# A conv-and-attention pair on one core: sampled keys copied by ScalarE, PSUM pools in another order, first queries copied by bank, one store moved on GpSimd's queue

## The chip, the cores and the metric

The kernel runs on one core of one Trainium2 chip. A core has four compute engines that run at the same time, each through its own list of instructions in order: TensorE (PE in the profile; its weight loads are shown as PEld), VectorE (DVE), ScalarE (ACT) and GpSimd (POOL). SyncE (SP) issues DMA transfers; GpSimd and ScalarE also issue some. The engines wait for each other through semaphores. Matmul results land in PSUM, a small memory of eight banks, from which VectorE or ScalarE has to copy ("evict") them.

The metric is the device time of one execution, in microseconds (us), as the median of several runs. Lower is better.

## What is computed

All numbers are float32. The input x has shape (2, 512, 32, 32). Two layers follow each other. The first is a deformable attention with an MLP behind it:

```python
xn  = bn(x, bn1_g, bn1_b)
q   = gconv1x1(xn, qw)                              # 8 groups of 64 channels
off = depthwise_conv6x6(q, stride=4)                # 8 x 8 positions for each image and group
off = tanh(pointwise(gelu(off + b), 2)) * 4
kv  = grid_sample(xn, grid + off)                   # 64 sampled keys for each image and group
k, v = gconv1x1(kv, kw), gconv1x1(kv, vw)
pos  = sign(d) * log1p(abs(d)),  d = grid_q - grid_kv          # 1024 queries x 64 keys x 2
bias = relu(relu(pos @ w1 + b1) @ w2 + b2) @ w3 + b3           # an MLP of width 128
x  = x + out_w @ (softmax(q k / 8 + bias) v) + out_b
x  = x + mlp_w2 @ gelu(mlp_w1 @ bn(x, bn2_g, bn2_b) + b) + b
```

The second layer is plain attention over the 1024 positions with 512 channels (Wq, Wk, Wv, Wp), added to x. By far the most work is the bias: an MLP with a hidden layer of 128 x 128 for every pair of a query and a key, 16 times over (two images, eight groups).

## The kernel before

**Opening.** A few matmuls on zeros (`wake`, L147) keep TensorE busy until the first input is there. Then the first 128 channels go through `chain(0)`: the batch norm on ScalarE (L264), the queries on TensorE into a PSUM tile `psq` of two banks (L270), and four copies of them into `qa` (L276). Output groups are numbered f = 0, 1 and lie in bank f; halves of the pixels h = 0, 1 lie in the upper and lower 64 partitions. VectorE then applies the 36 taps of the strided convolution (L308, L310), ScalarE the GELU (L342), TensorE the pointwise product (L354), ScalarE the tanh (L364). The features of the positions (`fe`) go to DRAM (`fdr`, L405, issued by SP) and come back broadcast to all partitions (`fb`, L579, issued by SP right behind it). From `fb` ScalarE and VectorE make the tables `ta` and `tb` (L590, L596), and from these VectorE makes `h`, the first hidden layer of the bias MLP (L610).

Meanwhile TensorE multiplies weights of the second layer with each other (`weights`, L533). The products are copied by ScalarE into `gs` (L539) and stored to DRAM by a DMA of 1 MB that GpSimd issues (`gdr`, L540). `rank`, `order` and `arrange` sort the hidden units by the sign of their last weight; the last part of it is a handful of very small GpSimd operations on `sc`, `w3f` and `w3u` (L242 to L248).

**Main loop.** 256 steps follow, each for four keys of one group. In a step TensorE computes four blocks of the second hidden layer (L627, eight matmuls each, operands `h` and `cw`). Each block lies in one tile of the PSUM pool `zp`, which has three buffers of two banks. ScalarE evicts the blocks with a ReLU (`rx` at L634, `ua`, `uo` or `ub` at L636), VectorE adds them in pairs (L644), accumulating DMAs issued by GpSimd and copies issued by SP add them further (L646, L658, L661, L663), and once in four steps TensorE multiplies the sums by the last layer (L692) into a tile of the PSUM pool `simp` (two buffers of one bank). VectorE makes `h` two steps ahead, in three buffers.

**Behind the loop.** One slice of other work is put into each step: the generator `later()` yields the rest of `chain` and `sample` for the other channels, and its slices are placed behind the second eviction of the step with `issue_after`. `sample(ci)` computes the sampled keys, eight times in all. ScalarE makes interpolation weights (L446, L449) and scales the batch-norm bias in place (L452), VectorE multiplies the weights (L454), and TensorE sums over the pixels into `pkv`, which is a tile of `zp` like the blocks (L462). VectorE evicts `pkv` in four operations with the batch-norm scale and bias, which also put the keys into the order in which the loop takes them (L475). TensorE then makes k and v from `kv` (`pkk` at L482, `pkv` at L484), and ScalarE copies these (L488, L490). A scheduler reorders instructions between engines by their dependencies, so the order on each engine is that of the built program, and not always that of the text.

**Afterwards.** The output projection (`project`, L872) uses `zp`. Then the pools `simp` and `zp` are closed and a pool `mq` of four buffers of two banks takes all eight banks for the MLP (L925) and the second layer (L1056, L1154).

The change touches these lines:

```python
zpp, simpp = (tc.tile_pool(name=n, bufs=c, space=PSUM) for n, c in (("zp", 3), ("simp", 2)))     # L132
copy = nc.vector.tensor_copy if ci == 0 and h == 1 else nc.scalar.copy                           # L275
nc.vector.scalar_tensor_tensor(                                                                  # L475
    d[:, e], v[:, e], bns[r, k : k + 1], u[:, e], ALU.mult, ALU.add)
nc.gpsimd.dma_start(out=gdr[i], in_=gs[:, i])                                                    # L540
```

Of the kernel before, what the change touches and what calls it, by code (L numbers as in the profile page):

```python
# [8 lines left out]
F32 = mybir.dt.float32  # L9
AF = mybir.ActivationFunctionType  # L10
ALU = mybir.AluOpType
AX = mybir.AxisListType
PSUM = bass.MemoryType.PSUM

P = 128
# [4 lines left out]
J = 64  # L20
# [26 lines left out]
def conv_seq_kernel(ctx: ExitStack, tc: tile.TileContext, x, xt, kst, pst, cst, vec, wsm, outw, w1, w2, wl, wlt, brow, out):  # L47
    nc = tc.nc
# [11 lines left out]
    def col(name, i=0):  # L60
        return vs[:, VOFF[name] + i : VOFF[name] + i + 1]

    bns = cp.tile([P, 8], F32, name="bns")
# [65 lines left out]
        x = [q[:, k : k + 2, n : n + 512] for k in (0, 2) for n in (0, 512)]  # L129
        return w + [wsum[:, j] for j in range(3)], x + [parts[:, j] for j in range(3)]  # L130

    zpp, simpp = (tc.tile_pool(name=n, bufs=c, space=PSUM) for n, c in (("zp", 3), ("simp", 2)))  # L132
    zp, simp = zpp.__enter__(), simpp.__enter__()

    def flat(name):
        return zp.tile([P, 2, 512], F32, tag="ps2", name=name).rearrange("p h n -> p (h n)")
# [3 lines left out]
    ph = php.__enter__()  # L140
    with tc.tile_pool(name="lp", bufs=2) as lp:


        def wake(src, n):
            ps = flat("wake")
            for _ in range(n):
                nc.tensor.matmul(ps[0:32, 0:512], src[:, 0:32], src[:, 0:512], start=True, stop=True)  # L147


        edge = ph.tile([P, 2], F32, name="edge")  # L150
# [7 lines left out]
        for n in range(2):  # L158
            idle = lp.tile([P, 4 * HW], F32, tag="h1", name="idle", bufs=3)
            nc.gpsimd.memset(idle[:, 0:512], 0.0)  # L160
            wake(idle, n + 1)
        cs = ph.tile([P, 202], F32, name="cs")
        ws = ph.tile([P, 1408], F32, name="ws")
        wq, wk = ws[:, 0:512], ws[:, 512:1024]
# [85 lines left out]
        def newest(engine):  # L250
            return next(i for i in reversed(nc.cur_bb.bb.instructions) if i.engine == engine)
# [4 lines left out]
        def chain(ci):  # L256
# [3 lines left out]
            for i in range(K):  # L260
                k = k0 + i
                if i == 0:
                    xn = xn0.pop()
                nc.scalar.activation(xn, xn, AF.Identity, bias=col("bn1b", k), scale=bns[:, k : k + 1])  # L264
                if ci > 0:
                    yield
                ps = flat("psq")

                for f_, h_, f, h in QUADS:
                    nc.tensor.matmul(  # L270
                        ps[h_, f * 512 : (f + 1) * 512], wq[f_, k * P + 64 * f : k * P + 64 * f + 64],
                        xn[f_, h * 512 : (h + 1) * 512], start=True, stop=True,
                    )
                for f_, h_, f, h in QUADS:
                    copy = nc.vector.tensor_copy if ci == 0 and h == 1 else nc.scalar.copy  # L275
                    copy(qa[f_, b, k, h * 512 : (h + 1) * 512], ps[h_, f * 512 : (f + 1) * 512])  # L276
                if i + 1 < K:
                    xn = load(b, k + 1)
                elif ci + 1 < len(CHAINS):
                    xn0.append(load(*CHAINS[ci + 1][0]))  # L280
                yield
# [29 lines left out]
            else:  # L311


                for m in range(3):
# [9 lines left out]
                    for y0, y1, t0, t1 in rows:  # L324
                        for k in range(K) if y1 - y0 < 8 else (slice(0, K),):
                            src, dst = pr[:, t0:t1, k, y0:y1, :], acc[:, m, k, y0:y1, :]
# [87 lines left out]
        def sample(ci):  # L414
            G = CHAINS[ci]
            K = len(G)
            th = state[ci]
            gx = th[:, 0:2].rearrange("p i g j -> p (i g j)")

            nc.vector.tensor_scalar(gx, gx, 1.0, 16.0, ALU.add, ALU.mult)  # L420
            if ci > 0:
                yield


            sg = ph.tile([P, 5, 2, K * J], F32, tag="fe", name="sg")
            hat = sg[:, 0:4].rearrange("p a f j -> p (a f j)")[:, 0 : 4 * K * J]
            nc.scalar.activation(hat, gx, AF.Abs, bias=edge[:, 0:1])
            nc.scalar.activation(hat, hat, AF.Relu, bias=edge[:, 1:2])
            nc.scalar.activation(hat, hat, AF.Relu, bias=1.0, scale=-1.0)
            yield  # L430
            nc.vector.tensor_tensor(sg[:, 4], sg[:, 0], sg[:, 1], ALU.mult)
            hx = ph.tile([P, 2, K, J], F32, tag="hx", name="hx")
            hxf = hx.rearrange("p f k j -> p (f k j)")
            nc.scalar.activation(hxf, th[:, 0].rearrange("p g j -> p (g j)"), AF.Abs, bias=hb[:, 0:1])
            nc.scalar.activation(hxf, hxf, AF.Relu, bias=1.0, scale=-1.0)
            yield
            gy = th[:, 1].rearrange("p (f k) j -> p f k j", f=2)
            for i, (b, k) in enumerate(G):
                g = b * NCH + k
                xnt = ph.tile([P, 8, P], F32, name="xnt")  # L440
                nc.sync.dma_start(out=xnt, in_=xt[:, b, k])
                wt = ph.tile([P, 8, 2, J], F32, name="wt")
                for t in range(8):
                    if t == 4:
                        yield
                    nc.scalar.activation(wt[:, t], gy[:, :, i, :], AF.Abs, bias=hb[:, 1 + t : 2 + t])  # L446
                yield
                wtf = wt.rearrange("p t f j -> p (t f j)")
                nc.scalar.activation(wtf, wtf, AF.Relu, bias=1.0, scale=-1.0)  # L449
                for f in range(2):  # L450
                    r, v = slice(64 * f, 64 * f + 64), sg[:, 4, f, i * J : (i + 1) * J]
                    nc.scalar.activation(v[r], v[r], AF.Copy, scale=col("bn1b", k)[r])  # L452
                yield
                nc.vector.tensor_tensor(  # L454
                    wt, wt, hx[:, :, i, :].unsqueeze(1).to_broadcast([P, 8, 2, J]), ALU.mult
                )
                yield
                ps = flat("pkv")
                for t in range(8):
                    for f in range(2):  # L460
                        r = slice(64 * f, 64 * f + 64)
                        nc.tensor.matmul(  # L462
                            ps[r, 0:J], xnt[:, t, r], wt[:, t, f, :], start=(t == 0), stop=(t == 7)
                        )
                kv = ph.tile([P, J], F32, name="kv")

                for f in range(2):
                    r = slice(64 * f, 64 * f + 64)
                    d = kv[r].rearrange("p (e i t) -> p e i t", e=2, t=8)
                    v, u = (  # L470
                        t[r].rearrange("p (i e t) -> p e i t", e=2, t=8)
                        for t in (ps[:, 0:J], sg[:, 4, f, i * J : (i + 1) * J])
                    )
                    for e in range(2):
                        nc.vector.scalar_tensor_tensor(  # L475
                            d[:, e], v[:, e], bns[r, k : k + 1], u[:, e], ALU.mult, ALU.add
                        )
                yield


                ps, pk = flat("pkv"), flat("pkk")
                nc.tensor.matmul(pk[:, 0:J], wk[:, k * P : (k + 1) * P], kv, start=True, stop=True)  # L482
                for f_, h_, f, h in QUADS:
                    nc.tensor.matmul(  # L484
                        ps[h_, f * 512 : f * 512 + 256], kv[f_, :], uo[f_, k, h * 256 : (h + 1) * 256],
                        start=True, stop=True,
                    )
                nc.scalar.activation(kz[:, g], pk[:, 0:J], AF.Copy, scale=DH ** (-0.5))  # L488
                for f_, h_, f, h in QUADS:
                    nc.scalar.copy(vp[f_, g, h * 256 : (h + 1) * 256], ps[h_, f * 512 : f * 512 + 256])  # L490
                yield
            state[ci] = None
# [34 lines left out]
        def weights(i):  # L527
            ps = [flat("psg") for _ in range(2)]
            for o in range(NCH):
                for k in range(NCH):  # L530
                    if i == 0 and (o, k) in ((1, 0), (3, 1)):
                        yield
                    nc.tensor.matmul(  # L533
                        ps[k // 2][:, k % 2 * 512 : k % 2 * 512 + 512], wls[i][:, 0, o, k * P : (k + 1) * P],
                        wls[i][:, 1, o, :], start=(o == 0), stop=(o == NCH - 1),
                    )
            yield
            for k2 in range(2):
                nc.scalar.copy(gs[:, i, 2 * k2 : 2 * k2 + 2, :].rearrange("p k o -> p (k o)"), ps[k2])  # L539
            nc.gpsimd.dma_start(out=gdr[i], in_=gs[:, i])  # L540


        PE = mybir.EngineType.PE
# [14 lines left out]
        for _ in head:  # L558
            pass
        with tc.issue_after(newest(mybir.EngineType.Activation)):  # L560
            next(g, None)
        with tc.issue_after(newest(PE)):
            arrange()
        with tc.issue_after(newest(PE)):
            next(n)
        next(n, None)


        NS = NG * NSL
# [274 lines left out]
    with ExitStack() as top, tc.tile_pool(name="wp", bufs=2) as wp:  # L844
# [164 lines left out]
        project(1, *op1, op1w[:, 3:5].rearrange("p a k n -> p a (k n)"))  # L1009
        spread([xb[:, j] for j in range(7)])  # L1010
        load_unit(*units[1])
        for pl in (simpp, zpp):
            pl.__exit__(None, None, None)
        mqp = tc.tile_pool(name="mq", bufs=4, space=PSUM)
        mq = mqp.__enter__()
# [326 lines left out]
```

## Time and profile before

| What | Value |
| --- | --- |
| Median of 3 runs | 2685.91 us (2681.35 to 2688.14) |
| Time of the profiled execution | 2688.11 us |
| Its span, first to last instruction | 2686.3 us |
| Mean granted TensorE clock | 0.997 |
| PE, DVE, ACT, POOL busy | 99%, 84%, 63%, 21% of the span |
| Main loop on PE (L627) | 1789.6 us busy, 16384 records |
| Eviction of the keys (L475) | 32 operations, 0.25 us each |

How to read it: a profile names for each instruction its engine, its line in the kernel, and its tiles as output<-input. In lists of waits, the columns are the total idle time of the engine, how often, and the longest. "PEclk" is the share of full speed that TensorE's clock was granted. A line in order of time gives the start and the length in us, then the instruction, how many records are merged in it (a float32 matmul has two), and in brackets the idle time of the engine just before it and what ended that.

### The profile page before, as it was taken

How to read it: one execution, taken by the hardware profiler on the slowest of the kernel's cores; microseconds unless marked ns; L12 is line 12 of the kernel's file. 1: busy time of each engine (PE TensorE's matmuls, PEld its weight loads, DVE VectorE, ACT ScalarE, POOL GpSimd, SP SyncE). 2: the span in 40 equal slices, each digit the busy share in tenths (PEclk: the TensorE clock that was granted, in tenths of full speed). 3: DMA queues.
4: the chain of work that ended last, by engine and by line, in shares of the span. 5: the costliest groups of instructions: out<-in, count | busy, mean ns of one | idle time of the engine just before them, and what ended most of it. 6: DMA issues, size and time to landing. Idle time of an engine off the chain costs nothing.

```text
span 2686.3 us, 46913 instructions
## 1 busy us (share of the span) xinstructions
PE 2663.3 (99%) x19596; PEld 960.0 (36%) x19596; DVE 2249.2 (84%) x1353; ACT 1688.3 (63%) x2193; POOL 576.9 (21%) x615
## 2 busy tenths in 40 slices
PE   9999999999999999999999999999999999999999
PEld 3343322332332333233323333333344444446455
DVE  6999999999999999999999999999774484466354
ACT  4787898788978888877777777777621131114041
POOL 1222222222222222222222222222243222000000
PEclk9999999999999999999999999999999999999999
DMA  5766766767666766666766776776631110000000
GB/s 197 150 150 145 163 139 141 158 140 157 147 147 142 153 144 142 145 140 142 150 146 146 149 150 142 151 149 145 153 123 47 47 47 33 15 16 0 32 0 32
DMA packets 96131, 316.67 MB, mean 118 GB/s; under 512 B 17104, under 2 KB 19424, under 8 KB 93232
## 3 DMA queue, kind: packets, MB, share of 16 engines
q0 software_dynamic: 57312, 202.26, 40.4%
q1 hardware_dynamic: 38176, 111.10, 11.6%
q8 instruction: 155, 2.54, 0.4%
q14 instruction: 56, 0.46, 0.0%
q10 hardware_dynamic: 432, 0.31, 0.0%
HBM read 74.28 MB, written 6.55 MB: 30 GB/s over the span
## 4 chain that ended last, share of the span: by engine, by line
PE 83%; DVE 6%; issue 5%; DMA 3%; ACT 2%; POOL 1%; DVEq 0%; SPq 0%; POOLq 0%; ACTq 0%
PE ps L627 52%; PE sw L925 14%; PE sw L1056 9%; DVE h L610 3%; PE sw L1154 2%; PE sim L692 2%; DMA ua<-ua 1%; DMA ua<-uo 1%; PE psg L533 1%; DVE ub L644 1%; PE sw L872 1%; DVE uo L644 1%; DVE ua L644 0%; ACT rx L634 0%; DMA wr<-in_wlt 0%
## 5 line engine op out<-in xcount | busy, mean ns | idle before, releaser
L627 PE MATMUL ps<-h,cw 128*32 128x512 f32 x16384 | 1789.6, 593 | 11.5 <-DVE kv L475 8.6
L610 DVE CUSTOM_DVE_ANT_1 h<-ta,tb 128x4096 f32<-128x4096 f32 (+1 forms) x257 | 1131.8, 4405 | 48.9 <-PE ps L627 45.0
L627 PEld LDWEIGHTS ps<-h,cw 128*32 128x32 f32 x16384 | 541.2, 110 | 1225.0 <-issue 1155.7
L634 ACT ACTIVATE rx<-ps,sc 128x1024 f32<-128x1024 f32 x512 | 568.3, 1110 | 177.2 <-PE ps L627 158.8
L636 ACT ACTIVATE ub<-ps,sc 128x1024 f32<-128x1024 f32 x256 | 308.2, 1204 | 97.2 <-PE ps L627 97.1
L644 DVE SCALAR_TENSOR_TENSOR ub<-rx,sc,ub 128x1024 f32<-128x1024 f32 x256 | 327.5, 1279 | 6.0 <-ACT ub L636 5.7
L646 POOL DMA_DIRECT2D ua<-ub x128 | 115.5, 903 | 730.4 <-DVE ub L644 703.3
L925 PE MATMUL sw<-xb,w1t 128*128 128x512 f32 x448 | 196.7, 600 | 3.1 <-DVE xs L123 3.1
L925 PE MATMUL sw<-hm,w2t 128*128 128x512 f32 x448 | 193.6, 592 | 0.0
L646 POOL DMA_DIRECT2D uo<-ub x127 | 117.0, 921 | 356.6 <-DVE ub L644 316.1
L636 ACT ACTIVATE ua<-ps,sc 128x1024 f32<-128x1024 f32 x128 | 154.1, 1204 | 54.6 <-PE ps L627 54.3
L663 POOL DMA_DIRECT2D ua<-uo x126 | 110.6, 878 | 352.5 <-DMA ua<-uo 350.7
L636 ACT ACTIVATE uo<-ps,sc 128x1024 f32<-128x1024 f32 x128 | 154.1, 1204 | 48.7 <-PE ps L627 45.9
L644 DVE SCALAR_TENSOR_TENSOR ua<-rx,sc,ua 128x1024 f32<-128x1024 f32 x128 | 163.7, 1279 | 13.7 <-ACT ua L636 13.7
L644 DVE SCALAR_TENSOR_TENSOR uo<-rx,sc,uo 128x1024 f32<-128x1024 f32 x128 | 163.8, 1280 | 7.8 <-ACT uo L636 7.7
L123 DVE TENSOR_TENSOR hm<-hm,sw 128x1024 f32<-128x1024 f32 x56 | 67.5, 1219 | 107.2 <-PE sw L925 106.9
L658 POOL DMA_DIRECT2D ua<-ua x126 | 153.8, 1221 | 1.6 <-issue 1.6
L925 PEld LDWEIGHTS sw<-xb,w1t 128*128 128x128 f32 x448 | 86.1, 193 | 112.6 <-issue 106.4
L934 ACT ACTIVATE hm<-hm,vs 128x512 f32<-128x512 f32 x64 | 42.6, 714 | 129.0 <-DVE hm L123 129.0
L925 PEld LDWEIGHTS sw<-hm,w2t 128*128 128x128 f32 x448 | 85.1, 190 | 107.1 <-issue 106.7
L123 DVE TENSOR_TENSOR xs<-xs,sw 128x1024 f32<-128x1024 f32 (+1 forms) x48 | 55.6, 1171 | 72.0 <-PE sw L1056 36.0
L1056 PE MATMUL sw<-aT,vt 128*128 128x512 f32 x224 | 96.7, 593 | 0.3 <-ACT aT L1136 0.3
(238 smaller groups left out, 1799.0 us busy)
## 6 DMA issues: line engine op xcount, KB each, us to landing
ua<-ub POOLq DMA_DIRECT2D x128, 512.0 KB, 4.9
uo<-ub POOLq DMA_DIRECT2D x127, 512.0 KB, 5.2
fb<-fdr SPq DMA_DIRECT2D x64, 512.0 KB, 5.2
ua<-ua POOLq DMA_DIRECT2D x126, 256.0 KB, 6.4
ua<-uo SPq DMA_DIRECT2D x126, 256.0 KB, 2.6
ua<-uo POOLq DMA_DIRECT2D x126, 256.0 KB, 3.8
w1t<-in_w SPq DMA_DIRECT2D x8, 1024.0 KB, 4.7
w2t<-in_w SPq DMA_DIRECT2D x8, 1024.0 KB, 4.7
```

Source lines behind the costliest of these rows:

```text
L123: nc.vector.tensor_tensor(out, a, b_, op)
L610: nc.vector._custom_dve(TENSOR_ADD_SAT, out=h1[:, y : y + step].rearrange("p y t x -> p (y t x)"), in0=a.unsqueeze(1).to_broadcast([P, ste ...
L627: nc.tensor.matmul(ps[32 * q : 32 * q + 32, h, :], cw2[:, 32 * z : 32 * z + 32], h1[:, 16 * h : 16 * h + 16, q, :], start=True, stop=True,)
L634: nc.scalar.activation(o, ps, AF.Relu, bias=sc[:, 4 + z : 5 + z])
L636: nc.scalar.activation(o, ps, AF.Relu, bias=sc[:, 4 + z : 5 + z], scale=sc[:, z : z + 1])
L644: nc.vector.scalar_tensor_tensor(r[1], r[0], sc[:, z : z + 1], r[1], ALU.mult, ALU.add)
L646: nc.gpsimd.dma_start(out=sums[s][1], in_=sums[s][3], accum_op=ALU.add)
L658: nc.gpsimd.dma_start(out=lanes(s, 0), in_=lanes(s, 1), accum_op=ALU.add)
L663: nc.gpsimd.dma_start(out=lanes(s, 1), in_=lanes(s + 1, 0), accum_op=ALU.add)
L692: nc.tensor.matmul(sims[gi][q : q + 32, :], w_, t[:, h, :], start=(i == 0 and f == 0), stop=(i == NSL // 4 - 1 and m == len(parts[e]) - 1),)
L925: nc.tensor.matmul(ps[:, m, :], w[:, a, k, m * P : (m + 1) * P], x[:, b_, k, :], start=(k == 0), stop=(k == 1),)
L1056: nc.tensor.matmul(ps[:, m, :], w[:, a, k, c + m * P : c + (m + 1) * P], x[b_][:, k, :], start=(k == 0), stop=(k == nk - 1),)
```

## The change

1. **Sampled keys.** `pkv` is now copied out of PSUM by one ScalarE operation with the batch-norm scale, for all 128 partitions at once and already in the loop's order. The scaled bias goes to a tile of its own, `uv`, in the same order, and one VectorE addition of 128 x 64 puts the two together.
2. **PSUM pools.** `simp` is opened before `zp` and closed after it, so that `simp` lies in the first two banks and `zp` in the other six.
3. **First queries.** Of the four copies out of `psq`, ScalarE takes those of f = 0 (bank 0), and VectorE those of f = 1 (bank 1). Before, the engines were split by h.
4. **Wake.** The last of the three matmuls on zeros has 256 columns in place of 512.
5. **G to DRAM.** `weights` yields once more before the DMA, so that the first `gdr` store stands on GpSimd's queue behind five of the seven small operations of `arrange`, just before the last two (L246). The second store stays where it was.

```diff
-    zpp, simpp = (tc.tile_pool(name=n, bufs=c, space=PSUM) for n, c in (("zp", 3), ("simp", 2)))
-    zp, simp = zpp.__enter__(), simpp.__enter__()
+    simpp, zpp = (tc.tile_pool(name=n, bufs=c, space=PSUM) for n, c in (("simp", 2), ("zp", 3)))
+    simp, zp = simpp.__enter__(), zpp.__enter__()
...
-        def wake(src, n):
+        def wake(src, *sizes):
             ps = flat("wake")
-            for _ in range(n):
-                nc.tensor.matmul(ps[0:32, 0:512], src[:, 0:32], src[:, 0:512], start=True, stop=True)
+            for n in sizes:
+                nc.tensor.matmul(ps[0:32, 0:n], src[:, 0:32], src[:, 0:n], start=True, stop=True)
...
-            wake(idle, n + 1)
+            wake(idle, *((512,), (512, 256))[n])
...
-                    copy = nc.vector.tensor_copy if ci == 0 and h == 1 else nc.scalar.copy
+                    copy = nc.vector.tensor_copy if ci == 0 and f == 1 else nc.scalar.copy
...
+                kv, uv = (ph.tile([P, J], F32, name=name) for name in ("kv", "uv"))
+                rowwise, natural = "p (e i t) -> p e i t", "p (i e t) -> p e i t"
                 for f in range(2):
                     r, v = slice(64 * f, 64 * f + 64), sg[:, 4, f, i * J : (i + 1) * J]
-                    nc.scalar.activation(v[r], v[r], AF.Copy, scale=col("bn1b", k)[r])
+                    nc.scalar.activation(
+                        uv[r].rearrange(rowwise, e=2, t=8), v[r].rearrange(natural, e=2, t=8), AF.Copy,
+                        scale=col("bn1b", k)[r],
+                    )
...
-                kv = ph.tile([P, J], F32, name="kv")
-
-                for f in range(2):
-                    r = slice(64 * f, 64 * f + 64)
-                    d = kv[r].rearrange("p (e i t) -> p e i t", e=2, t=8)
-                    v, u = (
-                        t[r].rearrange("p (i e t) -> p e i t", e=2, t=8)
-                        for t in (ps[:, 0:J], sg[:, 4, f, i * J : (i + 1) * J])
-                    )
-                    for e in range(2):
-                        nc.vector.scalar_tensor_tensor(
-                            d[:, e], v[:, e], bns[r, k : k + 1], u[:, e], ALU.mult, ALU.add
-                        )
+                nc.scalar.activation(
+                    kv.rearrange(rowwise, e=2, t=8), ps[:, 0:J].rearrange(natural, e=2, t=8), AF.Copy,
+                    scale=bns[:, k : k + 1],
+                )
+                nc.vector.tensor_tensor(kv, kv, uv, ALU.add)
...
                 nc.scalar.copy(gs[:, i, 2 * k2 : 2 * k2 + 2, :].rearrange("p k o -> p (k o)"), ps[k2])
+            yield
             nc.gpsimd.dma_start(out=gdr[i], in_=gs[:, i])
...
         with tc.issue_after(newest(mybir.EngineType.Activation)):
+            next(g)
+        with tc.issue_after(newest(PE)):
+            arrange()
+        with tc.issue_after(newest(mybir.EngineType.Pool)):
             next(g, None)
         with tc.issue_after(newest(PE)):
-            arrange()
-        with tc.issue_after(newest(PE)):
             next(n)
-        next(n, None)
+        for _ in n:
+            pass
...
-        for pl in (simpp, zpp):
+        for pl in (zpp, simpp):
             pl.__exit__(None, None, None)
```

## The prediction

> **What bounds the kernel.** I read the page first: busy time per engine, then who waits for whom on TensorE, then TensorE's clock by stretch, then instructions in order of time around each wait.
>
> ```profile
> PE 2663.3 (99%) x19596; PEld 960.0 (36%) x19596; DVE 2249.2 (84%) x1353; ACT 1688.3 (63%) x2193; POOL 576.9 (21%) x615
> ```
>
> TensorE is busy for 99% of the 2686.3 us span, so a change that removes none of its matmuls can gain only where it is idle or slow. The list of its waits adds up to 18.3 us; the largest (total, times, longest):
>
> ```profile
> PE ps L627 <- DVE kv L475: 8.6, 3, 3.6
> PE sw L925 <- DVE xs L123: 3.1, 1, 3.1
> PE wake L147 <- POOL idle L160: 1.6, 1, 1.6
> PE ps L627 <- ACT rx L634: 1.7, 4, 0.6
> PE ps L627 <- DVE h L610: 1.1, 1, 1.1
> ```
>
> Nearly half of the idle time is three waits for VectorE's eviction of the sampled keys (L475). Next, the granted clock in five stretches (PE, weight loads, DVE, ACT, POOL busy; then PEclk, DMA share, GB/s): the three key waits, the first MLP product, the opening.
>
> ```profile
> 533.60:537.90 4.30, 2.04 (x21) 0.49 (x17) 4.22 (x7) 1.11 (x1) 0.37 (x1) 1.00 0.63 124
> 840.60:846.60 6.00, 3.23 (x20) 0.60 (x16) 5.19 (x7) 1.26 (x3) 0.90 (x1) 0.72 0.48 113
> 1147.90:1157.70 9.80, 6.21 (x36) 1.61 (x32) 5.93 (x7) 3.96 (x4) 2.49 (x3) 0.65 1.00 237
> 1987.30:1996.50 9.20, 6.07 (x8) 2.52 (x8) 2.38 (x4) 0.00 (x0) 2.72 (x3) 0.63 0.94 336
> 6.70:37.70 31.00, 31.00 (x123) 14.04 (x122) 17.29 (x62) 10.25 (x19) 5.46 (x13) 1.00 0.71 271
> ```
>
> A clock of 0.72 over 6.00 us is 3.4 us at half speed, 0.65 over 9.80 is 6.9, 0.63 over 9.20 is 6.8; the 2.26 us wait in the first stretch costs no clock. So a long wait is paid twice. Around 843 us, TensorE, then VectorE:
>
> ```profile
> 835.28 5.36 PE L627 MATMUL ps<-h,cw 128*32 128x512 f32 x48
> 843.41 3.32 PE L627 MATMUL ps<-h,cw 128*32 128x512 f32 x16 [2.77 <-DVE kv L475]
> 846.65 0.43 PE L482 MATMUL pkk<-kv,ws 128*128 128x64 f32 x2
> 838.06 4.41 DVE L610 CUSTOM_DVE_ANT_1 h<-ta,tb 128x4096 f32<-128x4096 f32 x1
> 842.51 0.84 DVE L475 SCALAR_TENSOR_TENSOR kv<-pkv,bns,sg 64x32 f32<-64x32 f32 x4
> ```
>
> The product `pkv` was ready at 835.4, but its eviction stands behind a 4.41 us layer-1 pass on VectorE, which runs without a gap; meanwhile `pkv` holds one of three PSUM buffers, so the fourth block of the next step waits.
>
> The opening, where the first queries lead to the first bias table:
>
> ```profile
> 6.73 1.09 PE L270 MATMUL psq<-xn,ws 64*64 64x512 f32 x8
> 25.30 0.70 SPq L405 DMA_DIRECT2D fdr<-fe  x1
> 25.52 0.65 POOL L540 DMA_DIRECT2D gdr<-gs  x1 [11.62 <-ACT sc L239]
> 34.65 1.45 ACT L590 ACTIVATE ta<-fb,vs 128x128 f32<-128x128 f32 x2 [9.20 <-DMA fb<-fdr]
> 35.37 8.83 DVE L610 CUSTOM_DVE_ANT_1 h<-ta,tb 128x2048 f32<-128x2048 f32 x3 [0.23 <-ACT ta L590]
> 37.71 1.06 PE L627 MATMUL ps<-h,cw 128*32 128x512 f32 x8
> 39.91 6.21 PE L627 MATMUL ps<-h,cw 128*32 128x512 f32 x56 [1.14 <-DVE h L610]
> ```
>
> TensorE has weight products (L533) until 37.7 and then waits 1.14 us for the second half of h.
>
> **The Trainium skill.** "TensorE: Matmul & The Clock Gate", Part 1: the array runs at half rate until a free-running window of about 3.4 us was busy. The trace agrees: 3.4 and 6.8 us of half clock, after idle gaps of 2.77 to 3.59 us. [...]The four L276 copies do alternate strictly here (7.89, 8.50, 9.23, 9.84 us). "DMA: Bandwidth & Descriptors", Queues, rings and completion order: each DMA engine takes turns between its queues by packet. Here the 32 KB `fdr` write took 5.7 us to land beside the 1 MB `gdr` write, 2.5 us at 479 us.
>
> **Part 1, sampled keys.** Removed, eight times: four VectorE ops (0.84 us). Added: one ScalarE scaled copy of 128x64 from PSUM and one VectorE add of 128x64. The copy resembles L488 (0.21 us) with a strided output, so 0.2 to 0.4 us, I take 0.3; the add is L338's 0.24 us. `uv` replaces an in-place copy at the same 0.34 us (L452). In the built order the ScalarE copy stands right behind the `ub` eviction of the step's fourth block, ahead of the next `rx`; that eviction ends 0.2 us or less after `pkv` and `rx` follows 1.3 us or more later, so nothing is held up. The PSUM buffer is then free some 1 us after `pkv`, and the fourth block no longer waits on VectorE. What waits next is L482, for the add, which keeps VectorE's old place. Per wait:
> - 536: the block starts at 535.97 - 2.26 = 533.71, lasts 1.86, so L482 comes at 535.57; the add is done at 535.07 + 0.24. L482 was at 537.83: 2.3 us.
> - 843: block 840.64 to 842.50; add done 842.75, L482 at 842.8 instead of 846.65: 3.85 us, with 0.3 us of new wait.
> - 1151: two blocks (3.58 us) from 1147.95, L482 at 1151.5 instead of 1157.74: 6.2 us.
>
> Sum 12.3 us, about 8.3 of it idle time and 4 half clock. The other five have no idle and no gain. Does VectorE's lag only move? After 1151 it has gaps of 3.96, 1.01 and 0.91 us (next h, uo, h) because TensorE was late; they absorb 5.9 us, and the 0.6 us saved on the keys most of the rest of 6.2. After 843 the gaps (0.94, 0.99, 0.91) and 0.6 cover 3.4 of 3.85, after 536 (0.63, 0.91) and 0.6 nearly the 2.3. Before they are absorbed, the next `rx` needs a sum finished 2.4 us earlier. So the lag fits; if that cover fails, up to half returns.
>
> **Part 2, the opening.** Wake: a half-clock pass of 512 columns starts each 0.855 us, two per matmul; halving the last matmul saves 0.86 us and ends the wake near 5.95. The queries then wait for `xn` (ready 6.24), so L270 starts near 6.3: 0.43 us earlier. The clock's window sees a new gap of 0.36 us; the window from 842.9 us held 0.55 us of idle and still brought full speed, so I expect full speed. Copies: ScalarE takes bank 0, VectorE bank 1, but in the built program VectorE's first copy still waits for ScalarE's second. Three handovers become one: about 0.1 us. TensorE reaches L354 at 19.5 and `gof` is ready at 19.4, so both shift: 0.45 us in all.
>
> `gdr` behind the sums: GpSimd's five ops (26.20 to 27.76, 1.56 us) start when the DMA issue's 0.65 us no longer stands ahead, near 25.05 with the shift; `gdr` is issued near 26.6 and its packets start some 1.3 us later, near 27.9. Two more GpSimd ops then end 0.3 us after the issue; their reader comes at 42. The `fdr` write, issued near 24.85, is alone: landing 2.5 us later, 27.4 against 31.0. Its reader `fb`, queued on SP right behind it, now shares the DMA engines with `gdr`: 3.65 us so far, later loads under traffic 4.1 to 6.4; so it lands at 31.5 to 33.8, I take 32.5, against 34.6. The second half of h ends 5.2 us after that, at 37.7; TensorE needs it at 37.25 + 1.06 = 38.3. So the 1.14 us wait goes too (0.6 of it at the late end). Opening: 1.6 us, between 0.5 and 1.7.
>
> **Part 3, PSUM order.** Simp's banks now lie where the first MLP product's buffer goes, but in the built program that product still waits for the second projection's last eviction, as before. The 3.1 us and the half clock after it stay: 0, with 6.2 as the upper bound if addresses matter.
>
> **Sum.** 12.3 + 1.6 = 13.9 us off the profiled execution's 2688.1 us (span 2686.3): 2674.2. That execution stands 2.2 us above the median 2685.91. The window's phase differs by run, so a median run probably loses less to half clock; there I take 8.3 + 1.6 + 2 = 11.9: 2674.0. Both give 2674; what a measurement of this kernel tells from no change is 0.3%, 8.1 us, that is 2677.9.
>
> **Rivals.**
> - VectorE's lag comes back at L482 or at `rx` evictions, because VectorE is busy without a gap before each wait: half of part 1 is lost, 2680 (2679 to 2683). Against it: the gaps above. 0.14.
> - Cold start: the shorter wake misses its window; TensorE runs 3.4 or 6.8 us more at half clock, 1.7 to 3.4 us: 2676 to 2678. 0.08.
> - The pool order does free the first MLP product: 2668. Against it: the wait in the built program. 0.05.
> - Slower: VectorE's add waits for ScalarE, and behind the add stand both sums and h for every later step. The ScalarE copy is ready 2.5 us (106 and 884 us) to 7.5 us before VectorE comes. If `ub` evictions ahead of it are held by an unfinished accumulating DMA, all lateness over 2.5 us stalls VectorE, at worst eight times; from about 22 us in all (2.7 us each) the kernel is slower: 2695 and more. The page shows no such hold at these points. 0.05.
>
> The forecast itself: 0.68, range 2671 to 2677.5. With the cases: faster by over 0.3%: 0.65 + 0.05 + half the cold start, 0.75; within: 0.20; slower 0.05. The range of 2668 to 2681 leaves out the slower case, a worse lag, and some below 2668.
>
> **What will show it.** Right: no TensorE wait on `kv` but one of about 0.3 us near 839; clock 1.00 through the sampling; `fdr` landing within 3 us; no wait before the second half of h; 3.1 us still before the first MLP product; a list of TensorE's waits near 9 us. Wrong: new waits on `rx`, `h` or L482 of over 1 us, VectorE idle before the add, `fb` later than 34, or half clock beyond 7 us.

## The result, and the profile after

The changed kernel takes 2674.0 us (median of 5 runs, 2672.5 to 2674.62) against 2685.91 us (5 runs, 2681.35 to 2688.76): a ratio of 0.9956, with a 95% interval of 0.9941 to 0.9970. That is 11.9 us less, and the spread of single executions shrank from 7.4 to 2.1 us. The profiled execution took 2672.5 us, with a span of 2670.7 us, 15.6 us shorter than the one before. Lines behind L475 moved by one or two: the blocks of the loop are L629, the MLP L927, the sums' last product L694, and `pkk` and `pkv` are L480 and L482.

The first line of the page (busy time of each engine, share of the span, instructions):

```profile
PE 2654.7 (99%) x19596; PEld 959.0 (36%) x19596; DVE 2243.1 (84%) x1329; ACT 1690.1 (63%) x2201; POOL 575.5 (22%) x615
```

TensorE has 8.6 us less to do with the same instructions, which is what half clock had cost (17.1 us of it, at half speed). VectorE lost 24 instructions (32 evictions gone, 8 additions come) and ScalarE gained 8.

TensorE's list of waits (total, times, longest), the lines that matter:

```profile
PE sw L927 <- DVE xs L123: 3.0, 1, 3.0
PE ps L629 <- ACT rx L636: 1.6, 4, 0.6
...
PE sim L694 <- DMA ua<-uo: 1.2, 1, 1.2
...
PE psq L270 <- ACT xn L264: 0.5, 1, 0.5
...
PE pkk L480 <- DVE kv L475: 0.4, 1, 0.4
```

The three waits for the keys (8.6 us) and the one for the second half of h (1.1 us) are gone. The MLP's wait (first line) stands as it stood, and the four on `rx` too. Three lines are new: 1.2 us for an accumulating DMA, 0.5 before the queries, and 0.4 for the keys' addition.

Stretches of time around the former waits (PE, weight loads, DVE, ACT, POOL busy; then granted clock, DMA share, GB/s): the three key waits, the first MLP product.

```profile
533.00:538.00 5.00, 5.00 (x48) 1.64 (x44) 5.00 (x5) 3.35 (x8) 1.76 (x2) 1.00 0.65 126
838.00:842.00 4.00, 3.62 (x38) 1.18 (x34) 4.00 (x5) 2.90 (x7) 0.89 (x1) 1.00 0.34 90
1143.00:1153.00 10.00, 8.54 (x82) 2.63 (x75) 8.89 (x5) 7.17 (x15) 2.65 (x3) 1.00 0.83 212
1976.00:1990.00 14.00, 12.14 (x29) 5.44 (x30) 5.16 (x7) 2.30 (x2) 9.07 (x8) 1.00 0.70 255
```

The clock is full in all four, where the prediction's stretches at the last three places had 0.72, 0.65 and 0.63. In the fourth the wait is still there (12.14 busy of 14.00), but in this execution no half clock followed.

Around 839 us, the place that the prediction showed at 843; TensorE, then ScalarE and VectorE, in order of time:

```profile
830.46 1.15 PE L468 MATMUL pkv<-wt,xnt 128*64 128x64 f32 x32
831.54 7.07 PE L629 MATMUL ps<-h,cw 128*32 128x512 f32 x64
838.99 0.41 PE L480 MATMUL pkk<-kv,ws 128*128 128x64 f32 x2 [0.38 <-DVE kv L475]
```

```profile
831.70 0.30 ACT L471 ACTIVATE kv<-pkv,bns 128x64 f32<-128x64 f32 x1
...
834.30 4.41 DVE L612 CUSTOM_DVE_ANT_1 h<-ta,tb 128x4096 f32<-128x4096 f32 x1
838.64 0.21 DVE L475 TENSOR_TENSOR kv<-kv,uv 128x64 f32<-128x64 f32 x1
```

The four blocks behind `pkv` (64 records) now run through; before, the third of them was followed by a wait. ScalarE begins to empty `pkv` 0.1 us after it is done; VectorE's addition still stands behind the same 4.41 us pass, 6.6 us after the copy, but now only `pkk` waits for it, 0.38 us.

The opening, as in the prediction:

```profile
6.53 1.31 PE L270 MATMUL psq<-xn,ws 64*64 64x512 f32 x8 [0.50 <-ACT xn L264]
25.33 0.70 SPq L405 DMA_DIRECT2D fdr<-fe  x1
27.04 0.67 POOL L539 DMA_DIRECT2D gdr<-gs  x1
33.30 1.45 ACT L592 ACTIVATE ta<-fb,vs 128x128 f32<-128x128 f32 x2 [7.82 <-DMA fb<-fdr]
37.68 7.09 PE L629 MATMUL ps<-h,cw 128*32 128x512 f32 x64
```

`gdr` is issued 1.5 us later and `fdr` lands 2.2 us after its issue (5.7 before). `fb`, which now shares the time with `gdr`, takes 5.7 us in place of 3.65, but still lands earlier, at 33.27 (34.63 before). The first 64 records of the loop run without the break after eight.

How much the change gained up to each `pkk`, from its start in the two traces:

| `pkk` before, us | after, us | gained so far | step |
| --- | --- | --- | --- |
| 114.04 | 112.68 | 1.36 | opening 1.36 |
| 537.83 | 534.00 | 3.83 | first key wait 2.47 |
| 846.65 | 838.99 | 7.66 | second 3.83 |
| 1157.74 | 1143.58 | 14.16 | third 6.50 |
| 1202.54 | 1189.57 | 12.97 | DMA wait at 1146: 1.2 lost |

The first MLP product starts 12.6 us earlier (1990.46 and 1977.86). The rest to 15.6 us comes behind it: before, that wait was followed by 6.8 us of half clock, which is 3.4 us lost, and here by none.

### The profile page after: what moved, and what is told of

Read it like the earlier page. It is cut to its first block, busy times and chain, and to the rows that moved or that the text cites. A ratio compares the mean times of both kernels' runs of the same rounds, so it can differ in the third digit from the quotient of the medians.

```text
span 2670.7 us, 46906 instructions
## 1 busy us (share of the span) xinstructions
PE 2654.7 (99%) x19596; PEld 959.0 (36%) x19596; DVE 2243.1 (84%) x1329; ACT 1690.1 (63%) x2201; POOL 575.5 (22%) x615
## 4 chain that ended last, share of the span: by engine, by line
PE 84%; DMA 5%; issue 4%; DVE 4%; ACT 2%; POOL 1%; DVEq 0%; SPq 0%; POOLq 0%; ACTq 0%
PE ps L629 53%; PE sw L927 14%; PE sw L1058 9%; DMA ua<-ua 2%; DMA ua<-uo 2%; PE sw L1156 2%; PE sim L694 2%; DVE h L612 1%; PE psg L531 1%; DVE ub L646 1%; PE sw L874 1%; ACT rx L636 0%; POOL ua L665 0%; DVE xs L882 0%; DVE ua L646 0%
## 5 line engine op out<-in xcount | busy, mean ns | idle before, releaser
L629 PE MATMUL ps<-h,cw 128*32 128x512 f32 x16384 | 1784.8, 592 | 1.7 <-ACT rx L636 1.6
L629 PEld LDWEIGHTS ps<-h,cw 128*32 128x32 f32 x16384 | 541.1, 110 | 1210.6 <-issue 1155.0
L927 PE MATMUL sw<-xb,w1t 128*128 128x512 f32 x448 | 193.7, 592 | 3.0 <-DVE xs L123 3.0
L927 PE MATMUL sw<-hm,w2t 128*128 128x512 f32 x448 | 193.6, 592 | 0.0
L123 DVE TENSOR_TENSOR hm<-hm,sw 128x1024 f32<-128x1024 f32 x56 | 67.6, 1219 | 105.1 <-PE sw L927 104.7
L927 PEld LDWEIGHTS sw<-xb,w1t 128*128 128x128 f32 x448 | 85.0, 190 | 110.5 <-issue 105.0
L927 PEld LDWEIGHTS sw<-hm,w2t 128*128 128x128 f32 x448 | 85.1, 190 | 107.1 <-issue 106.2
L123 DVE TENSOR_TENSOR xs<-xs,sw 128x1024 f32<-128x1024 f32 (+1 forms) x48 | 55.6, 1171 | 72.9 <-PE sw L1058 36.0
```

The costliest lines, as they stand in the source:

```text
L123: nc.vector.tensor_tensor(out, a, b_, op)
L629: nc.tensor.matmul(ps[32 * q : 32 * q + 32, h, :], cw2[:, 32 * z : 32 * z + 32], h1[:, 16 * h : 16 * h + 16, q, :], start=True, stop=True,)
L927: nc.tensor.matmul(ps[:, m, :], w[:, a, k, m * P : (m + 1) * P], x[:, b_, k, :], start=(k == 0), stop=(k == 1),)
```

## The experiments

The theory is the prediction's: three separate gains (keys, store order, opening), of which the keys carry nearly all; the PSUM order nothing. The rival for the keys is that fewer VectorE operations, and not the engine, make the difference. Two more experiments put the remaining wait before the MLP to the test.

**The keys alone.** The kernel before with the three key edits, that is `uv`, ScalarE's copy and VectorE's addition, and nothing else:

```diff
...
-                        nc.vector.scalar_tensor_tensor(
-                            d[:, e], v[:, e], bns[r, k : k + 1], u[:, e], ALU.mult, ALU.add
-                        )
+                nc.scalar.activation(
+                    kv.rearrange(rowwise, e=2, t=8), ps[:, 0:J].rearrange(natural, e=2, t=8), AF.Copy,
+                    scale=bns[:, k : k + 1],
+                )
+                nc.vector.tensor_tensor(kv, kv, uv, ALU.add)
```

> The kernel before with part 1 alone (sampled keys by ScalarE). Theory (TensorE waited for the PSUM buffer that VectorE's queue kept): all three waits on kv go, about 11.5 us off, near 2675 us, and the wait of 1.1 us before the second half of h stays. Rival (the gain came from the opening, or from the phase of the clock): no more than 5 us off, 2681 us or later.

Measured: 2676.12 us (5 runs, 2675.43 to 2676.78) beside 2685.09 for the kernel before on the same chip, a ratio of 0.9961 (0.9948 to 0.9973). From its list of TensorE's waits:

```profile
PE sw L923 <- DVE xs L123: 2.8, 1, 2.8
...
PE ps L625 <- DVE h L608: 1.1, 1, 1.1
...
PE sim L690 <- DMA ua<-uo: 0.9, 1, 0.9
PE pkk L480 <- DVE kv L475: 0.6, 1, 0.6
```

The key waits are gone and the wait for h is not, so these two parts are separate. The new DMA wait is there as well (0.9 us, at 1147.9): it belongs to the keys' part. In its profiled execution 3.4 us of half clock followed the MLP's wait. The keys alone gain 9.0 us between medians, where the whole change gains 11.9.

**All but the keys.** The changed kernel with VectorE's four evictions back (the diff above reversed).

> The changed kernel with VectorE's four key operations put back, all else changed. Theory: the three kv waits of 2.3 to 3.6 us are back with half clock after the longer ones; only the opening's 1.4 us are gained, near 2684 us. Rival (the other parts carry the gain): near 2676 us.

Measured: 2683.76 us (21 runs, 2680.45 to 2687.57), a ratio of 0.9993 (0.9987 to 1.0000) to the 2685.09 of that chip. Its largest wait:

```profile
PE ps L631 <- DVE kv L475: 8.1, 3, 3.6
```

The three waits are back at 1.78, 2.75 and 3.59 us. All other parts together gain 1.3 us in the median, at the edge of what can be told from nothing; with the 9.0 of the keys alone that makes 10.3 of 11.9, within what these intervals (6.7 and 3.5 us wide) can tell.

**Only the store moved.** The kernel before with the extra `yield` in `weights` and the new places of its slices.

> The kernel before with the first gdr store behind GpSimd's sums, nothing else. Theory (fdr shared the DMA engines with gdr): fdr lands within 2.5 us instead of 5.7, fb near 33.3 us, the wait of 1.1 us before the second half of h is gone, 1.1 to 1.4 us off in the first main steps; three kv waits as before. Rival (the gain in the opening came from wake and copies): fdr still 5 us or more, wait of 1.1 us unchanged.

Measured: 2683.77 us (21 runs, 2680.44 to 2688.51), a ratio of 0.9995 (0.9989 to 1.0002): not told apart from no change by time, but plain in the trace. Its opening in order of time, and a stretch around the first key wait:

```profile
24.93 0.70 SPq L405 DMA_DIRECT2D fdr<-fe  x1
26.64 0.66 POOL L541 DMA_DIRECT2D gdr<-gs  x1
27.18 7.52 SPq L583 DMA_DIRECT2D fb<-fdr  x2
37.29 7.08 PE L631 MATMUL ps<-h,cw 128*32 128x512 f32 x64
```

```profile
533.60:538.00 4.40, 3.77 (x18) 0.89 (x18) 3.19 (x6) 0.14 (x1) 1.76 (x2) 0.61 0.39 74
```

`fdr` landed 2.2 us after its issue, `fb` at 32.87, and the wait for the second half of h is gone: this edit alone is the cause. The last line is a surprise: the same 2.26 us key wait that cost no clock before is followed here by 3.4 us at half clock (a mean of 0.61 over 4.40 us). The last section shows why.

**Only the wake and the copies.** The kernel before with the 256-column last wake matmul and the copies by bank.

> The kernel before with the shorter wake and the copies by bank, nothing else. As recorded in the prediction: 0.45 us earlier at the first weight products and at L354. Rival after seeing the changed kernel (the queries start before the clock rises and run at half rate, so nothing is left): L354 within 0.1 us of the kernel before, time the same within its interval, and the 1.1 us wait before the second half of h unchanged.

Measured: 2683.28 us (13 runs, 2681.17 to 2686.65), a ratio of 0.9993 (0.9985 to 1.0001) to the kernel before on its chip (2686.54). TensorE's opening:

```profile
5.40 0.63 PE L147 MATMUL wake<-idle 128*32 128x256 f32 x1
6.33 1.26 PE L270 MATMUL psq<-xn,ws 64*64 64x512 f32 x8 [0.29 <-ACT xn L264]
7.52 0.70 PE L533 MATMUL psg<-wl_s 128*128 128x512 f32 x1
```

The queries start 0.40 us earlier than before (6.73) and take 1.26 us in place of 1.09, so the weight products behind them gain only 0.23. The clock's record in the traces tells why: it rose to full at 6.74 us here, at 7.03 in the changed kernel, at 6.59 before. The moment of the rise differs between executions, 5.07 to 7.60 us over the ten profiled ones: 5.54 to 7.60 with the shorter wake and 5.07 to 7.28 without, so it does not come sooner because the queries do. Compared at like moments, L354 starts 0.12 us earlier with the wake and copies than without (19.58 with the rise at 7.03, the changed kernel; 19.70 with 6.99, the keys alone) 0.23 earlier (19.32 with 6.74, here; 19.55 with 6.59, before), and 0.09 earlier where both rises came well ahead of the queries (19.09 with 5.99, all but the keys; 19.18 with 5.07, only the store). This is about the size of the part. The wait before the second half of h was 0.85 us here, where the recorded rival had it unchanged at 1.1: `fb` landed 0.58 us earlier (34.05 and 34.63), 0.23 by the earlier issue of `fdr` and the rest because `fb` itself took 3.3 us and not 3.65.

**Only the PSUM order.**

```diff
-    zpp, simpp = (tc.tile_pool(name=n, bufs=c, space=PSUM) for n, c in (("zp", 3), ("simp", 2)))
+    simpp, zpp = (tc.tile_pool(name=n, bufs=c, space=PSUM) for n, c in (("simp", 2), ("zp", 3)))
...
```

> The kernel before with the PSUM pools opened and closed in the other order, nothing else. Theory (the first MLP product waits for the second projection's last eviction wherever its buffer lies): wait of 3.0 to 3.1 us there unchanged, time unchanged. Rival (the address frees it): that wait is gone, 3 to 6 us off.

Measured: 2685.5 us (21 runs, 2681.01 to 2687.97) beside 2686.54, a ratio of 0.9995 (0.9988 to 1.0002). The first MLP product:

```profile
1990.88 2.93 PE L925 MATMUL sw<-xb,w1t 128*128 128x512 f32 x3 [2.95 <-DVE xs L123]
```

It still waits, 2.95 us (3.13 before), and the time is the same within its interval. No effect of the order of the pools shows.

**The keys by VectorE in two operations.** The changed kernel, but `pkv` is emptied by two VectorE operations over all 128 partitions instead of ScalarE's copy and the addition. This has fewer VectorE operations than before and keeps the engine.

```diff
-                nc.scalar.activation(
-                    kv.rearrange(rowwise, e=2, t=8), ps[:, 0:J].rearrange(natural, e=2, t=8), AF.Copy,
-                    scale=bns[:, k : k + 1],
-                )
-                nc.vector.tensor_tensor(kv, kv, uv, ALU.add)
+                for e in range(2):
+                    nc.vector.scalar_tensor_tensor(
+                        kv.rearrange(rowwise, e=2, t=8)[:, e], ps[:, 0:J].rearrange(natural, e=2, t=8)[:, e],
+                        bns[:, k : k + 1], uv.rearrange(rowwise, e=2, t=8)[:, e], ALU.mult, ALU.add,
+                    )
```

> The changed kernel with the keys evicted by VectorE in two operations of 128 x 32 (with uv as the bias), so that VectorE has little more to do than in the changed kernel but the eviction stands in its queue again. Theory (the place in the queue counts): the three TensorE waits on kv are back at 2 to 3.5 us each, only some 0.3 us shorter than before, near 2683 us. Rival (the four operations' length counts): within 1 us of the changed kernel, near 2674 us.

Measured: 2681.02 us (10 runs, 2679.44 to 2684.02), a ratio of 0.9984 (0.9974 to 0.9993) to 2685.09. TensorE, then VectorE, around the second wait:

```profile
833.27 5.36 PE L629 MATMUL ps<-h,cw 128*32 128x512 f32 x48
840.74 2.65 PE L629 MATMUL ps<-h,cw 128*32 128x512 f32 x16 [2.12 <-DVE kv L472]
```

```profile
835.95 4.42 DVE L612 CUSTOM_DVE_ANT_1 h<-ta,tb 128x4096 f32<-128x4096 f32 x1
840.29 0.40 DVE L472 SCALAR_TENSOR_TENSOR kv<-pkv,bns,uv 128x32 f32<-128x32 f32 x2
```

The eviction got 0.44 us shorter and still stands behind the h pass; the block still waits 2.12 us for it (2.77 before, with all else of the change 2.75). The three waits are 1.70, 2.12 and 3.03 us, which is 0.08, 0.63 and 0.56 us shorter than with the four operations (some 0.3 was expected). So the length of the operations is worth about 2.7 us (2683.76 to 2681.02), and who does the eviction about 7 (2681.02 to 2674.0, on two chips). The rival covers the smaller part.

**The row sums out of the way.** In front of the first MLP product, VectorE's last eviction of the second projection (L123) stands behind a row sum of `wr` (L1034) that waits for its load. In the changed kernel the row sums are issued behind VectorE's newest instruction:

```diff
-            nc.vector.scalar_tensor_tensor(
-                wr, wr, 1.0, br, ALU.mult, ALU.mult, accum_out=ub[:, j, k : k + 1]
-            )
+            with tc.issue_after(newest(mybir.EngineType.DVE)):
+                nc.vector.scalar_tensor_tensor(
+                    wr, wr, 1.0, br, ALU.mult, ALU.mult, accum_out=ub[:, j, k : k + 1]
+                )
```

> The changed kernel with VectorE's row sums (L1034, which wait for a load of wr) issued behind VectorE's newest instruction, so that they no longer stand ahead of the second projection's last eviction. Theory (that eviction, about 1.4 us late behind such a sum, holds the first MLP product): the wait of 3.0 us falls to 1.6 to 1.9, the clock stays full after it, 1 to 3 us off, near 2672 us. Rival (the eviction waits for its own matmuls, not for the sum): wait unchanged, time unchanged.

Measured: 2670.37 us (5 runs, 2669.95 to 2670.44), a ratio of 0.9939 (0.9926 to 0.9951) to 2686.54. It is below every run of the changed kernel. VectorE in the changed kernel, before the first MLP product:

```profile
1975.97 0.69 DVE L1034 SCALAR_TENSOR_TENSOR wr<-wr,br 128x512 f32<-128x512 f32 x1 [0.65 <-DMA wr<-in_wlt]
...
1976.59 1.22 DVE L123 TENSOR_TENSOR xs<-xs,sw 128x1024 f32<-128x1024 f32 x1
```

And in this one:

```profile
1974.37 1.22 DVE L123 TENSOR_TENSOR xs<-xs,sw 128x1024 f32<-128x1024 f32 x1 [0.68 <-PE sw L874]
```

The last eviction now waits for nothing but its own product. The first MLP product waits 1.31 us (2.98 before) and starts at 1975.64 (1977.86): 2.2 us. The medians differ by 3.6, which leaves 1.4. All five executions have a mean clock of 1.000, where four of the five of the changed kernel have 0.999; a half-clock stretch of 3.4 us would cost 1.7 us, about what is left. That it is the stretch behind the MLP's wait is argued from the other traces, since those four executions have no trace.

**The wait filled.** The changed kernel with three matmuls of 512 columns into an unread tile of `simp`, between the second projection and the first MLP product: TensorE is busy and the wait remains.

```diff
+        fill = simp.tile([P, 512], F32, name="sim")
+        for _ in range(3):
+            nc.tensor.matmul(fill, xb[:, 0, 0, 0:P], xb[:, 0, 0, :], start=True, stop=True)
```

> The changed kernel with three additional matmuls of 512 columns into a PSUM tile that nobody reads (2.6 us at full clock), placed between the second projection and the first MLP product, where TensorE idles for 3.0 us. Theory (idle time there costs half clock in some executions, by the window's phase): the first MLP product starts no later, its clock stays at 1.000 in every execution, median 0.5 to 2 us below the changed kernel, executions within 1 us of each other. Rival (clock dips do not matter): same median as the changed kernel; or later by up to 2.6 us if the matmuls are not hidden.

Measured: 2674.22 us (5 runs, 2672.18 to 2679.56), a ratio of 0.9957 (0.9945 to 0.9970). TensorE there:

```profile
1974.93 2.74 PE L1014 MATMUL sim<-xb 128*128 128x512 f32 x6
1978.16 1.10 PE L927 MATMUL sw<-xb,w1t 128*128 128x512 f32 x2 [0.49 <-PE sim L1014]
```

The fill does what it was put there for (0.49 us left), and the product starts 0.3 us later than in the changed kernel. But the median is no lower, and two of the five executions took 2677.49 and 2679.56 us at a clock of 0.999, above every run of the changed kernel. What happened in these two has no trace and stays open. The experiment is inconclusive on whether the half clock behind this wait explains the spread of the changed kernel.

## Why the prediction was right

It gave 2674.0 us within 2668 to 2681; the median is 2674.0. The mechanism of each large part held. That the median came out to the tenth is luck: the terms below are off by up to 3 us, in both directions, and nearly cancel. Step by step:

**Keys, 12.3 us: right.** The three events gained 2.47, 3.83 and 6.50 us against 2.3, 3.85 and 6.2. The copy took 0.30 to 0.32 us (0.3), the addition 0.20 to 0.22 (0.24), and the new wait at 839 us was 0.38 (0.3). ScalarE began six of the eight copies 0.1 us after `pkv` and two 0.5 us after it, and VectorE was never idle before the addition, so the slower rival has nothing behind it.

**VectorE's lag, absorbed: right in its terms, with a cover missed beside them.** No wait on h appeared, and that of L629 on `rx` stayed at 1.6 us in four pieces. The first rival predicted 2680 and did not come. But TensorE's lateness at 1151 us had covered something that the step did not look at: the chain of accumulating DMAs that makes the sums. Here is TensorE, then GpSimd, after the change:

```profile
1143.58 0.43 PE L480 MATMUL pkk<-kv,ws 128*128 128x64 f32 x2
1144.25 0.66 PE L482 MATMUL pkv<-vp,kv 64*64 64x256 f32 x8 [0.23 <-ACT rx L636]
1146.13 0.62 PE L694 MATMUL sim<-ua,w3f 128*32 128x512 f32 x1 [1.22 <-DMA ua<-uo]
```

```profile
1140.46 0.84 POOL L665 DMA_DIRECT2D ua<-uo  x1 [2.13 <-DMA ua<-uo]
```

And the same two before it, GpSimd first:

```profile
1147.77 0.85 POOL L663 DMA_DIRECT2D ua<-uo  x1 [1.69 <-DMA ua<-uo]
...
1158.69 0.62 PE L692 MATMUL sim<-ua,w3f 128*32 128x512 f32 x1
```

The last DMA of the chain is issued at 1140.46 and lands 5.6 us later, near 1146.1; TensorE comes for its result at 1144.9. Before, it was issued at 1147.77, took 5.8 us, and was read at 1158.69, some 5 us after landing. Removing 6.5 us of lateness used up these 5 us, and 1.2 were paid back. The 12.3 is net about 11.6 in this execution. The waits in the output projection grew by another 0.5 us (L874 waits 1.9 us in two pieces, L872 1.4 before); the runs do not show why.

**Store order, the 1.14 us wait: right.** `fdr` landed after 2.2 us (2.5), `fb` at 33.27 (31.5 to 33.8, taken 32.5), and the wait is gone. The experiment with this edit alone shows it to be the cause. "DMA: Bandwidth & Descriptors" of the Trainium skill, Queues, rings and completion order, has each DMA engine take turns between its queues; the two landing times of the same 32 KB write, 5.7 us beside the 1 MB store and 2.2 without it, agree with that.

**Wake and copies, 0.45 us: mis-sized.** At like moments of the clock's rise they are worth 0.09 to 0.23 us, and in the profiled execution 0.03 were left by the time of the first block. The step that failed is "so I expect full speed": the start of the queries moved ahead of the rise of the clock, and the part of them that lies there runs at half speed, so about half of the 0.4 us comes back. Even with the rise where the trace before has it, 6.59 us, queries that start at 6.3 run partly at half speed, and the rise moves between executions. The copies by bank gave little: all four still follow one another (7.92, 8.51, 9.13 and 9.82 us in the changed kernel's trace), also where ScalarE and VectorE read different banks, and they end 2.60 us after they start, 2.65 before.

**"The 2.26 us wait in the first stretch costs no clock": phase, not size.** The same wait cost 3.4 us of half clock in two other profiled executions (below).

**Half clock in the median sum, 2 us: mis-sized.** In the five traces with VectorE's four operations on the keys, 6.8 or 10.2 us of half clock followed the three key waits, which is 3.4 or 5.1 us lost. So this term was too small by 1.4 to 3.1 us; the 1.2 us of the DMA wait, the 0.5 in the output projection and the smaller opening (1.36 in place of 1.6) are what it cancels against.

**PSUM order, 0: right,** by the experiment with that edit alone. The wait before the first MLP product stayed, 2.98 us; that 6.8 us of half clock behind it would stay too was wrong for the profiled execution. This put 3.4 us on its gain, about half of which the waits that came back took off again, and so it fell by 15.6 us and not by 13.9. The list of waits sums to 11 us in place of 9, mostly by the DMA wait and by 0.5 us each before the queries and in the output projection.

## What to carry to other kernels

When a small operation stands behind a long pass on its engine, making it shorter takes little off the wait (here 0.1 to 0.6 us for 0.44 us of length); giving the operation that frees the buffer to an engine with gaps removes it. Before taking out a wait, ask of every producer that the waiting engine reads next, DMA chains too, by how much it is ahead today: a lateness of 6.5 us had covered a DMA sum that was only 5 us ahead. And a wait of 2 us or more on TensorE should be priced as a chance of half clock behind it, over several executions, and not by the one that was profiled.

## What the runs showed of the hardware

**Half clock follows a short gap by its phase.** I set TensorE's idle gaps in the ten profiled executions (those of both kernels and eight experiments, start-up left out) beside the record of the granted clock. Seven gaps of 1.2 to 1.8 us were never followed by half clock. Of 17 gaps of 2.0 to 3.0 us, nine were followed by 3.4 us of half clock and eight by none: a gap of 2.03 us was followed, one of 2.98 was not. All seven gaps of 3.03 to 3.59 us were followed, three by 3.4 us and four by 6.8 us. "TensorE: Matmul & The Clock Gate" of the Trainium skill, Part 1, has the clock fall after at least one idle window of about 3.4 us; here gaps well shorter than that were enough, and the measurement decides.

The same records show what the phase is. In all ten traces every fall and rise of the clock lies a whole number of steps of 3.413 us behind the first rise: in the kernel before, the falls at 842.86, 1150.06 and 1989.73 us are 245, 335 and 581 steps behind 6.59. Cutting each trace into windows at these steps, I added up TensorE's idle time in each. All 16 windows at full clock with 2.03 us or more of it were followed by half clock, and no window at full clock with 1.94 us or less was. Two such windows and the one behind each, for the same 2.26 us wait, in the kernel before and then with only the store moved (length, PE busy, ...; then granted clock, DMA share, GB/s):

```profile
532.24:535.65 3.41, 1.47 (x16) 0.26 (x8) 3.36 (x4) 2.14 (x2) 0.13 (x1) 1.00 1.09 231
535.65:539.06 3.41, 3.09 (x27) 1.06 (x28) 3.38 (x5) 1.10 (x1) 1.53 (x2) 1.00 0.21 40
```

```profile
530.71:534.13 3.42, 1.27 (x12) 0.13 (x4) 3.37 (x5) 1.93 (x2) 0.00 (x0) 1.00 1.07 214
534.13:537.54 3.41, 3.31 (x16) 0.60 (x16) 2.53 (x3) 0.00 (x0) 1.75 (x2) 0.50 0.17 30
```

Before, the edge of a window cut the wait into 1.94 and 0.32 us, and the clock stayed full. With the store moved, 2.15 us of it fell into one window, and the next ran at half. The 2.98 us wait of the changed kernel's trace was cut into 1.64 and 1.34 us. With 2.0 us in one window as the limit, and a gap that falls anywhere in the windows with equal chance, an estimate follows: a gap of 2.0 us is followed by half clock in four executions of ten, one of 3.0 us in seven, and only one of some 4 us always. The 1.31 us that are left with the row sums moved are too short at any phase, by this count. Whether one or two windows run at half is not settled: 0.72 us or more of idle time reached into the first of them in the four cases of two, but 0.78 us in one case that stayed at one.

The same phase makes much of the spread. Of the kernel before, executions with a mean clock of 0.999 took 2680.7 to 2682.6 us, and those with 0.996 or 0.997 took 2684.9 to 2689.3. The spread was 7.4 us before, 2.1 after and 0.5 with the row sums moved, over five executions each; but it was 7.4 again with the wait filled, and so not all of it is the length of TensorE's waits.
